# Products that nobody reads on TensorE in front of the steps of a mixture-of-experts routing

## The chip, the cores and the metric

The kernel runs on one core of a Trainium2 chip. The metric is the device time of one execution, in microseconds (us). Five engines of the core work side by side, each through its own queue in order: TensorE (PE, with its weight loads as PEld), VectorE (DVE), ScalarE (ACT), GpSimd (POOL) and SyncE (SP, which issues most transfers). The profile also records the clock that was granted to TensorE, as a share of full speed.

## The reference, cut to what matters

The input is two images of 256 channels and 56 x 56 points. Two layers follow each other. Layer 0 is windowed attention and a mixture of experts, layer 1 two 3 x 3 convolutions with ternary weights and batch norms, and again a mixture of experts. The change stands between the convolutions and the experts of layer 1, where the 6272 points are tokens:

```python
x = x + _L1_conv_ref(_ln_c(x), ...)   # ends in relu(out1 + out2)
t = _to_tokens(x)
t = t + _L1_ffn_ref(_ln_t(t), ...)

def _L1_ffn_ref(x, gate_w, gate_b, W1, b1, W2, b2):
    logits = xf @ gate_w + gate_b            # 256 -> 8 experts
    probs = softmax(logits)
    top2_vals, top2_idx = top_k(probs, 2)
    # per expert: gelu(x W1 + b1) W2 + b2, 256 -> 512 -> 256, weighted and summed
```

## The kernel before

The image is worked in 14 strips of eight rows (`STRIPS`), 448 points each. For tokens, strips stand in groups of 128: an even strip has three groups, an odd one four (`groups_of`), 49 groups in all.

Layer 1's routing takes a strip through these steps, and an order written out by hand (`all_strips`) places the steps of three strips in each round, the new one `i`, the young one `i - 1` and the old one `i - 2`. The engines PE, DVE, ACT and SP keep that order.

- `residual(i)`: DVE scales and adds (line 2208), ACT applies the ReLU into `nr` (2211), PE transposes `nr` into the PSUM tile `pt` (2221), six or eight instructions. In the next round DVE adds the tokens kept from before (2225) and leaves the strip as tokens.
- `norm(i)`: DVE takes statistics of each token (739 to 749), ACT makes the normalised rows `u` (762), PE transposes `u` into `pu` (810), ACT copies that into `ut` (813), and PE multiplies `ut` with the gate into `pl` (822): 128 x 8 products, two instructions for each of the two halves of a group's channels, 12 or 16 a strip. In the next round DVE adds the gate's bias and has the logits `lgs` (831).
- `settle(batch)`: DVE finds the two best experts of each token (857 to 876), writes them as `hots` (882), and PE counts with a few small products into `rk` how many tokens came before to the same expert (892 to 895). In the next round DVE makes the places of the rows from it (904 to 911), and POOL scatters each group's rows into `xs` in DRAM, two indirect transfers a group (929). Strips 0 to 4 are settled one by one, the later ones two at a time: `BATCHES = [[0], [1], [2], [3], [4], [5, 6], [7, 8], [9, 10], [11, 12], [13]]`.

On PE the order of one round is therefore `pt` of the new strip, `rk` of the old one, `pu` and `pl` of the young one. On DVE it is 2225 and statistics of the young strip, places of the batch settled in the last round, 2208 of the new strip, then `lgs` and the choice for the old one.

POOL sends the rows of strips 0 to 8 within the stage. When these 31 groups are out, a tiny transfer on POOL's queue (`some`, 2236) serves as a fence; SP waits for it and then loads rows of `xs` as tiles `xg` (1129). The plan of the first expert tiles and the counting for the later ones (`counts`, 985) stand in the same order on PE and DVE. The experts follow: PE transposes `xg` (1150) and multiplies with the experts' weights (`ph`, 1182, and `py`, 1201).

The PSUM pool of the stage has two buffers of each tag: `aux` for `pu`, `rk` and counts (one bank each), `pl` (one bank each) and `pt` (two banks each).[...]

`all_w` is a constant 128 x 128 bf16 tile of ones.

Of the kernel before, what the change touches and what calls it, by code (L numbers as in the profile page):

```python
# [11 lines left out]
F32 = mybir.dt.float32  # L12
# [9 lines left out]
P = 128  # L22
# [19 lines left out]
E = 8  # L42
TT = NQ
NTT = NT // TT
# [30 lines left out]
def groups_of(i):  # L75

    at = 2 * NT // P * (i // 2) + NT // P * (i % 2)
    return at, NT // P + i % 2
# [13 lines left out]
def bcast(ap, axis, shape):  # L92
    return ap.unsqueeze(axis).to_broadcast(shape)
# [551 lines left out]
def metaformer(ctx: ExitStack, tc: tile.TileContext, a: dict, out: bass.AP, flag):  # L645
    nc = tc.nc
# [71 lines left out]
    all_w = const.tile([P, P], BF16, tag="all_w", name="all_w")  # L718
# [9 lines left out]
    def token_stats(tp, src, eps, root):  # L728

        rows, n = src.shape[0], src.shape[1]  # L730

        def small(name, *more):
            bufs = None if name == "t_stats" else 3
            t = tp.tile([P, NTT, *more], F32, tag=name, name=name, bufs=bufs)
            return t[:rows, :n]

        stats, mv = small("t_stats", 6), small("t_mv", 2)
        for t in range(n):
            nc.vector.bn_stats(stats[:, t, :], src[:, t, :])  # L739
        for t in range(n):  # L740
            nc.vector.bn_aggr(mv[:, t, :], stats[:, t, :])
        rstd, nmr = small("t_rstd"), small("t_nmr")
        nc.vector.tensor_scalar_mul(nmr, mv[:, :, 0], -1.0)
        if root:
            nc.scalar.activation(rstd, mv[:, :, 1], AF.Sqrt, bias=eps[:rows])
        yield
        if root:
            nc.vector.reciprocal(rstd, rstd)
            nc.vector.tensor_tensor(nmr, nmr, rstd, ALU.mult)
        else:  # L750
            nc.gpsimd.tensor_tensor(
                rstd, mv[:, :, 1], eps[:rows].to_broadcast([rows, n]), ALU.add
            )
            nc.gpsimd.tensor_tensor(rstd, rstd, minus_half[:rows, :n], ALU.pow)
            nc.gpsimd.tensor_tensor(nmr, nmr, rstd, ALU.mult)
            yield
            yield
        return rstd, nmr
# [13 lines left out]
    def routing(layer, wp, tp, ps):  # L772
# [10 lines left out]
        wgt = rt.tile([P, TOP, NGR], F32, tag="wgt", name="wgt", bufs=2)  # L783
# [3 lines left out]
        seen_b4 = wp.tile([P, E], BF16, tag="seen_b4", name="seen_b4")  # L787
        counted, sent, held_counts = [], [], []
        small_eng = nc.gpsimd if layer == 0 else nc.vector
        rows = {}  # L790

        def norm(i, src, late=False):


            eng = nc.vector if late else small_eng
            rstd, nmr = yield from token_stats(tp, src, eps5, layer == 1 or late)
            g0, ng = groups_of(i)
            row = tp.tile([P, NTT, RW], F32, tag="u", name="u", bufs=U_BUFS[layer])
            row = rows[i] = row[:, :ng]
            u = row[:, :, :C]  # L800
            if layer == 0 or i >= FIRST[1]:
                eng.memset(row[:, :, R_EX + 1 :], 0.0)
                eng.tensor_copy(row[:, :, R_ID], ids[:, g0 : g0 + ng])
            scaled(u, src, rstd, nmr)
            yield
            ut = tp.tile([P, KC, NTT * P], F32, tag="ut", name="ut", bufs=1)
            for k in range(KC):
                pu = ps.tile([P, 512], F32, tag="aux", name="pu")
                for t in range(ng):
                    nc.tensor.transpose(  # L810
                        pu[:, t * P : (t + 1) * P], u[:, t, k * P : (k + 1) * P], ident
                    )
                nc.scalar.copy(ut[:, k, : ng * P], pu[:, : ng * P])  # L813
            if layer == 0:
                eng.tensor_tensor(src, src, u, ALU.add)
                nc.sync.dma_start(by_token(x_mid, i), src)
                yield
            lg = lgs[:, g0 : g0 + ng, :]
            pl = ps.tile([P, NTT, E], F32, tag="pl" if layer else "aux", name="pl")[:, :ng]
            for t in range(ng):  # L820
                for k in range(KC):
                    nc.tensor.matmul(  # L822
                        pl[:, t, :],
                        ut[:, k, t * P : (t + 1) * P],
                        gate[:, k, :],
                        start=k == 0,
                        stop=k == KC - 1,
                    )
            if layer == 1:
                yield  # L830
                nc.vector.tensor_tensor(lg, pl, bcast(gate_b, 1, [P, ng, E]), ALU.add)
            else:
                nc.vector.tensor_copy(lg, pl)
            yield

        def settle(strips):
# [3 lines left out]
            n = sum(groups_of(i)[1] for i in strips)  # L840
# [47 lines left out]
            if strips[-1] == FIRST[layer] - 1:  # L888
                nc.vector.tensor_copy(seen_b4, seen)
                counted.append(True)  # L890
            rk = ps.tile([P, n, E], F32, tag="aux", name="rk")
            nc.tensor.matmul(rk, before_w, hots, start=True, stop=False)
            nc.tensor.matmul(rk, all_w, bcast(seen_b, 1, full), start=False, stop=n == 1)
            for t in range(n - 1):
# [4 lines left out]
                    start=False,  # L899
                    stop=t == n - 2,  # L900
# [182 lines left out]
            nc.vector.tensor_tensor(held, below, since, ALU.mult)  # L1083
            return where, held, name

        return norm, settle, tiles, planning, gates, wgt, counted, sent

    def experts(layer, FF, plans, ys, wp, tp, ps, at_tile=None):

# [208 lines left out]
    def ring(i):  # L1298

        at = P // 2 * (1 - i % 2)  # L1300
        return slice(at, at + NT)
# [124 lines left out]
    with ExitStack() as st:  # L1426
        aw = st.enter_context(tc.tile_pool(name="att_w", bufs=1, reuse_waits="tile"))
        tp = st.enter_context(tc.tile_pool(name="att_t", bufs=2, reuse_waits="tile"))
        ps = st.enter_context(tc.tile_pool(name="att_ps", bufs=2, space=PSUM, reuse_waits="tile"))
# [38 lines left out]
        for n in "vo":  # L1468
            rows = P if n == "o" else TT
# [26 lines left out]
        for i in range(3):  # L1496
            t = sw.tile([TT, NTT, PAIRS, 4, HD], F32, tag=f"vals{i}", name=f"vals{i}")
            nc.gpsimd.memset(t[:, :, :, 1:3, :], 1.0)
            vals.append(t)
        keys = {}  # L1500
        norm0, settle0, tiles0, _, gates0, wgt0, counted0, sent0 = routing(0, aw, tp, ps)

        def project(g):
            s = g % NS
# [334 lines left out]
    with mid:  # L1839

        with ExitStack() as st:
            rp = st.enter_context(tc.tile_pool(name="raw", bufs=1, reuse_waits="tile"))
            ps = st.enter_context(tc.tile_pool(name="conv_ps", bufs=4, space=PSUM, reuse_waits="tile"))
# [9 lines left out]
            tp = strips_on.enter_context(  # L1853
                tc.tile_pool(name="conv_t", bufs=2, side="right", reuse_waits="tile")
            )
# [322 lines left out]
        with ExitStack() as both:  # L2178
# [3 lines left out]
            wp = both.enter_context(  # L2182
                tc.tile_pool(name="route_w1", bufs=1, side="right", reuse_waits="tile")
            )
            tp = both.enter_context(
                tc.tile_pool(name="route_t1", bufs=2, side="right", reuse_waits="tile")
            )
            route_ps = ExitStack()
            ps = Banks(
                route_ps.enter_context(  # L2190
                    tc.tile_pool(name="route_ps1", bufs=2, space=PSUM, reuse_waits="tile")
                ),
                True,
            )
# [3 lines left out]
            def residual(i):  # L2198

                b, s = STRIPS[i]  # L2200
                r = X[b, s]
                ng = groups_of(i)[1]
                cols = ring(i)
                back = tp.tile([P, NTT, C], F32, tag="back", name="back", bufs=1)[:, :ng]
                nc.sync.dma_start(back, by_token(x_mid, i))
                for o in range(KC):
                    ro = r[:, o, :].rearrange("p (h w) -> p h w", w=W)
                    nc.vector.scalar_tensor_tensor(  # L2208
                        ro, ro, scale2[:, o : o + 1], inner(b, s)[:, :, o], ALU.mult, ALU.add
                    )  # L2210
                    nc.scalar.activation(
                        in_blocks(nr[:, o, cols]),
                        narrow(ro),
                        AF.Relu,
                        bias=shift2[:, o : o + 1],
                    )
                pt = ps.tile([P, NTT, C], F32, tag="pt", name="pt")[:, :ng]
                for t in range(ng):
                    at = in_ring(i, t)
                    for k in range(KC):  # L2220
                        nc.tensor.transpose(  # L2221
                            pt[:, t, k * P : (k + 1) * P], nr[:, k, at], ident
                        )
                yield
                nc.vector.tensor_tensor(XT[b, s], pt, back, ALU.add)  # L2225
# [2 lines left out]
                yield from residual(i)  # L2228
                yield from norm(i, XT[STRIPS[i]])

            norm, settle, tiles, planning, gates, wgt1, _, sent = routing(1, wp, tp, ps)

            def fence():

# [107 lines left out]
    with ExitStack() as st:  # L2342
        tp = st.enter_context(tc.tile_pool(name="last_t", bufs=2, reuse_waits="tile"))
        ps = st.enter_context(tc.tile_pool(name="last_ps", bufs=2, space=PSUM, reuse_waits="tile"))
        PT = 2
        outs = {}
        for i, (b, s) in enumerate(STRIPS):
            xt = XT[b, s]
            g0, ng = groups_of(i)
            outs[i] = tp.tile([P, KC, NT], F32, tag="out", name="o_out", bufs=6)  # L2350
            rows = by_token(ys[1], i, TOP)
            for t0 in range(0, ng, PT):
# [4 lines left out]
                for t in range(t0, t0 + m):  # L2357
                    n = g0 + t
# [148 lines left out]
```

## Time and profile before

| | us |
|---|---|
| median of three runs | 1736.08 (1735.79 to 1740.23) |
| the profiled execution | 1717.51 |
| its span in the profile | 1715.70 |
| last convolution's last product on PE starts | 1116.11 |
| routing of layer 1, up to the first transpose of the experts | 1118 to 1262.16 |
| experts of layer 1 | 1262 to 1655 |
| combining and output | 1655 to 1715.7 |

All times inside the profile are counted from the start of its span. A row of the timeline gives the start, the length, the engine, the line of the kernel, the operation, and in square brackets the idle time before it and what ended it. A row of stages or windows gives the stretch, its length, for PE, weight loads, DVE, ACT and POOL the busy time and the number of instructions, then TensorE's granted clock (1.00 is full), the busy share of the DMA engines and GB/s. A row of the waits says which engine and line waited for which, in us in total, how often, and the longest.

### The profile page before, as it was taken

The page shows a single profiled execution, that of the slowest core. Times are in us where ns is not written, and L with a number is a line of the kernel's source. Part 1 is how long each engine was busy: PE and PEld are TensorE (multiplying, and loading weights), DVE is VectorE, ACT ScalarE, POOL GpSimd, SP SyncE. Part 2 cuts the span into 40 slices and gives each one's busy share as a digit, 9 for nine tenths or more (in the row PEclk, how much of TensorE's full clock was granted, in tenths as well). Part 3 has the DMA queues.
Part 4 walks back from the last instruction along what each step waited for, and adds up shares of the span by engine and source line. Part 5 has one row for each costly group of instructions (what it writes and reads, how often), then busy time and mean ns, then how long its engine had stood idle before and what let it go on. Part 6 is the DMA issues. An engine that isn't in the chain of part 4 may idle for free. (4 is left out here: it accounts for less than half of the span.)

```text
span 1715.7 us, 25578 instructions
## 1 busy us (share of the span) xinstructions
PE 1494.3 (87%) x8445; PEld 1170.3 (68%) x8445; DVE 958.2 (56%) x2620; ACT 694.3 (40%) x1419; POOL 636.9 (37%) x729
## 2 busy tenths in 40 slices
PE   5999999899877979994989879957679999999964
PEld 3556565555556857783778778746578888898952
DVE  3456667466645445976998888777743112111136
ACT  2545443353433434553444263234433334343423
POOL 2112435243343773551333323427715542222210
PEclk9999998899889989996999989955579999999975
DMA  7122324121267877984441000024457877888858
GB/s 240 47 64 92 109 96 141 46 92 62 64 180 238 296 251 290 310 302 182 175 143 71 1 1 0 10 65 140 154 186 271 274 259 263 284 288 293 299 194 328
DMA packets 94189, 291.78 MB, mean 170 GB/s; under 512 B 20183, under 2 KB 35643, under 8 KB 84960
## 3 DMA queue, kind: packets, MB, share of 16 engines
q1 hardware_dynamic: 70384, 231.82, 40.9%
q0 software_dynamic: 19856, 51.82, 8.0%
q10 hardware_dynamic: 3808, 6.42, 1.0%
q8 instruction: 69, 1.13, 0.3%
q14 instruction: 72, 0.59, 0.1%
HBM read 218.55 MB, written 74.20 MB: 171 GB/s over the span
## 5 line engine op out<-in xcount | busy, mean ns | idle before, releaser
L1182 PE MATMUL ph<-ut,w 128*128 128x256 f32 (+1 forms) x1472 | 307.7, 360 | 13.0 <-DMA w<-in_L_experts 11.0
L1211 DVE TENSOR_TENSOR y<-py,w 128x512 f32<-128x512 f32 (+1 forms) x120 | 76.9, 640 | 403.8 <-PE py L1201 387.6
L1201 PE MATMUL py<-w,h 128*128 128x256 f32 x1288 | 298.3, 380 | 2.1 <-DVE y L1211 2.1
L1182 PEld LDWEIGHTS ph<-ut,w 128*128 128x128 f32 x1472 | 250.0, 194 | 41.6 <-DMA w<-in_L_experts 12.9
L1201 PEld LDWEIGHTS py<-w,h 128*128 128x128 f32 x1288 | 243.7, 191 | 35.0 <-DVE y L1211 2.5
L929 POOL DMA_INDIRECT xs<-u,pos x196 | 195.4, 997 | 114.7 <-issue 37.5
L1213 POOL DMA_INDIRECT ys<-y,dest x136 | 136.0, 1000 | 217.5 <-DVE dest L1157 94.8
L1189 ACT ACTIVATE h<-ph,w 128x256 f32<-128x256 f32 (+1 forms) x368 | 162.7, 448 | 110.0 <-PE ph L1182 104.5
L1592 ACT ACTIVATE ex<-sc 112x476 f32<-112x476 f32 (+3 forms) x224 | 116.8, 573 | 176.0 <-PE sc L1582 174.7
L1154 ACT COPY ut<-pt 128x512 f32<-128x512 f32 (+1 forms) x120 | 65.2, 543 | 272.8 <-PE pt L1150 272.8
L1923 PE MATMUL pc<-lo,wq 128*128 128x448 f32 x336 | 133.7, 400 | 5.7 <-DVE lo L1898 5.5
L1923 PE MATMUL pc<-hi,wq 128*128 128x448 f32 x336 | 132.5, 396 | 2.4 <-DVE x L1945 1.9
L1612 DVE TENSOR_TENSOR acc<-av,acc 128x238 f32<-128x238 f32 (+3 forms) x224 | 88.4, 408 | 77.4 <-PE av L1602 76.6
L1213 POOL DMA_INDIRECT ys<-y,to x81 | 81.6, 1008 | 121.3 <-DVE dest L1157 63.5
L1602 PE MATMUL av<-ex,vals 112*64 112x238 f32 (+3 forms) x896 | 122.8, 397 | 4.1 <-DVE acc L1612 4.1
L2066 PE MATMUL pc<-hi,wq 128*128 128x448 f32 (+1 forms) x288 | 102.9, 367 | 17.8 <-ACT hi L2033 9.4
L1573 PE MATMUL sc<-q_im,keys 32*112 32x238 f32 (+3 forms) x896 | 99.3, 426 | 8.7 <-ACT ex L1592 8.6
L2066 PE MATMUL pc<-lo,wq 128*128 128x448 f32 (+1 forms) x288 | 102.1, 364 | 0.2 <-DVE lo L2034 0.2
L1896 POOL TENSOR_TENSOR v<-pad 128x928 f32<-128x928 f32 (+1 forms) x28 | 56.8, 2041 | 105.1 <-ACT pad L1879 61.0
L1602 PEld LDWEIGHTS av<-ex,vals 112*64 112x64 f32 x896 | 56.1, 140 | 52.0 <-issue 27.9
L1150 PE MATMUL pt<-ident,xg 128*128 128x128 f32 x434 | 69.6, 281 | 21.6 <-DMA xg<-xs 17.9
L1573 PEld LDWEIGHTS sc<-q_im,keys 32*112 32x112 f32 x896 | 46.0, 175 | 49.7 <-ACT ex L1592 25.3
(279 smaller groups left out, 2477.3 us busy)
## 6 DMA issues: line engine op xcount, KB each, us to landing
w<-in_L_experts SPq DMA_DIRECT2D x64, 1154.0 KB
w<-in_L_experts SPq DMA_DIRECT2D x56, 641.0 KB
xg<-xs SPq DMA_DIRECT2D x97, 260.0 KB
acc<-in_fresh SPq DMA_DIRECT2D x14, 896.0 KB
got<-ys SPq DMA_DIRECT2D x21, 512.0 KB
got<-ys SPq DMA_DIRECT2D x7, 1024.0 KB
xt<-in_x_tok SPq DMA_DIRECT2D x14, 448.0 KB
rec<-shares SPq DMA_DIRECT2D x28, 224.0 KB
```

The costliest lines, as they stand in the source:

```text
L929: w = nc.gpsimd.indirect_dma_start(xs[:, :], bass.IndirectOffsetOnAxis(ap=pos[:, j, t0 + t : t0 + t + 1], axis=0), at_of[t][0][:, at_of[t] ...
L1182: nc.tensor.matmul(ph[:, :g], w1[:, k, f * P : (f + 1) * P], d["ut"][:, k, :g], start=k == 0, stop=k == KC - 1,)
L1189: nc.scalar.activation(d["h"][:, f, :g], ph[:, :g], AF.Gelu, bias=b1[:, f : f + 1])
L1201: nc.tensor.matmul(py[:, i, :], d["h"][:, f, i * P : (i + 1) * P], w2[:, f, :], start=f == 0, stop=f == NF - 1,)
L1211: nc.vector.tensor_tensor(y[:, :gp], py[:, :gp], bcast(b2, 1, [P, gp, C]), ALU.add)
L1213: o = nc.gpsimd.indirect_dma_start(ys[:, :], bass.IndirectOffsetOnAxis(ap=d["to"][:, i : i + 1], axis=0), y[:, i, :], None, bounds_check=T ...
L1573: nc.tensor.matmul(sc[h // 2][:, h % 2, :nq], keys[g][p, c, tx * TT : (tx + 1) * TT], q_im[p, c, r0:r1, c0:c1], start=True, stop=False,)
L1592: nc.scalar.activation(e[:, :, :nq], sc[j][:, :, :nq], AF.Exp, scale=HD**-0.5)
L1602: nc.tensor.matmul(av[VW * i : VW * (i + 1), :nq], vals[g % 3][:, tx, 2 * c + j, 2 * i : 2 * i + 2, :].rearrange("p a d -> p (a d)"), ex[j ...
L1612: added = nc.vector.tensor_tensor(d, av[:, :nq].rearrange("p (h w) -> p h w", w=c1 - c0), d, ALU.add)
L1923: nc.tensor.matmul(pc[:, :NT], wq[:, k, c, dx * C + o * P : dx * C + (o + 1) * P], part[:, :, k, dx : dx + W], start=m == 0, stop=m == 2 * ...
L2066: nc.tensor.matmul(pc[:, : 2 * ns * W], wq[:, k, c, dx * C + o * P : dx * C + (o + 1) * P], part[:, : 2 * ns, k, dx : dx + W], start=m == ...
```

## The change

Within layer 1's routing a helper `busy(n)` puts `n` products of `all_w` with itself, repeated to 512 columns, into PE's queue. They are written to a tile `spare` of one PSUM bank, which nobody reads. The helper is called in front of `pt` (30 for strip 0, 6 for each other strip), in front of `pu` (20 for strip 0, else 5), in front of `pl` (2), and in front of `rk` (12 for the first batch, else 4). To make room for the bank, `pl` has one buffer in place of two in layer 1. Layer 0 is left as it was. On the other four engines the instructions and their order are the same as before.

```diff
+        def busy(n):
+
+            if layer == 0:
+                return
+            if not spare:
+                spare.append(ps.tile([P, NTT, P], F32, tag="spare", name="spare", bufs=1))
+            for _ in range(n):
+                nc.tensor.matmul(
+                    spare[0], all_w, bcast(all_w, 1, [P, NTT, P]), start=True, stop=True
+                )
...
             scaled(u, src, rstd, nmr)
             yield
+            busy(5 if i else 20)
             ut = tp.tile([P, KC, NTT * P], F32, tag="ut", name="ut", bufs=1)
...
             lg = lgs[:, g0 : g0 + ng, :]
-            pl = ps.tile([P, NTT, E], F32, tag="pl" if layer else "aux", name="pl")[:, :ng]
+            busy(2)
+            if layer:
+                pl = ps.tile([P, NTT, E], F32, tag="pl", name="pl", bufs=1)[:, :ng]
+            else:
+                pl = ps.tile([P, NTT, E], F32, tag="aux", name="pl")[:, :ng]
...
+            busy(4 if strips[0] else 12)
             rk = ps.tile([P, n, E], F32, tag="aux", name="rk")
...
+                busy(6 if i else 30)
                 pt = ps.tile([P, NTT, C], F32, tag="pt", name="pt")[:, :ng]
```

## Prediction

> **What bounds the kernel now.** I read the page's forty slices first, then engine sums by stage, the granted clock in windows cut at its own edges, the timelines of TensorE (PE) and VectorE (DVE), and the waits. Slices:
>
> ```profile
> PE   5999999899877979994989879957679999999964
> PEclk9999998899889989996999989955579999999975
> ```
>
> Around slices 26 to 29 stands layer 1's routing, the one long stretch with a half clock and a half-filled PE. By stage (columns: length; busy PE, weight load, DVE, ACT, POOL; clock; DMA):
>
> ```profile
> 1118.00:1262.00 144.00, 90.69 (x452) 77.46 (x452) 106.40 (x434) 60.83 (x120) 74.58 (x154) 0.56 0.42 138
> 1262.00:1655.00 393.00, 389.56 (x2075) 346.82 (x2075) 70.62 (x257) 146.60 (x325) 138.61 (x141) 0.99 0.76 260
> ```
>
> The experts after it are PE from end to end at clock 0.99, so what the routing gains or loses moves the end of the kernel one for one. In the routing DVE is busier than PE. What DVE waits for, and how the stage ends:
>
> ```profile
> DVE lgs L831 <- PE pl L822: 12.9, 6, 4.8
> DVE x L2225 <- PE pt L2221: 5.0, 3, 1.7
> DVE counts L987 <- PE counts L985: 3.0, 1, 3.0
> ...
> 1247.36 0.61 POOL L2236 DMA_DIRECT2D some<-xs  x1 [7.17 <-DMA xs<-u,pos]
> ...
> 1252.96 4.78 SPq L1129 DMA_DIRECT2D xg<-xs  x5
> ...
> 1262.11 0.19 PE L985 MATMUL counts<-seen_all,all_w 128*128 128x8 bf16 x1 [0.88 <-DVE seen_all L983]
> 1262.16 1.95 PE L1150 MATMUL pt<-ident,xg 128*128 128x128 f32 x8
> ```
>
> So in the 112 us of the first three rows a faster PE can return at most 20.9 us. Two paths end in the first expert tile: the strip loop, whose last step (counts) lets PE go at 1262.1, and POOL's scattered rows, the fence and the loads of xg, issued at 1252.96 and, at 260 KB each, due about 1256. The strip loop is last, by some 6 us: gains beyond that are covered by POOL's path unless it starts earlier too.
>
> **What the clock follows.** Four windows of 3.41 us:
>
> ```profile
> 1184.19:1187.60 3.41, 3.41 (x18) 3.41 (x17) 0.98 (x2) 1.05 (x3) 2.61 (x6) 0.50 0.25 87
> 1187.60:1191.02 3.42, 1.93 (x14) 1.49 (x12) 3.35 (x12) 1.43 (x4) 2.84 (x6) 1.00 0.69 222
> 1191.02:1194.43 3.41, 1.80 (x6) 1.11 (x6) 2.96 (x16) 2.85 (x6) 2.83 (x9) 0.50 0.25 87
> ...
> 1163.71:1167.12 3.41, 3.41 (x18) 3.41 (x18) 1.39 (x7) 2.67 (x5) 2.83 (x6) 0.50 0.49 190
> ```
>
> Both 1163.7 and 1184.2 show PE busy throughout, but only the second is followed by the full clock. The first is mostly pl, matmuls of 8 columns; the second is transposes of 128. Counting moved columns only (pl is then 1/16 of a transpose), the windows of the routing that were followed by the full clock held 0.75 of activity or more, those that stayed low 0.60 or less, and the full clock was lost after windows of 0.08 or less; elsewhere in the trace it held from about 0.4 up and mostly went below that. That count is my estimate from shapes and times.
>
> The page "TensorE: Matmul & The Clock Gate" of the Trainium skill has two rules on this. Its closing table ("Why this matters for your kernels") says that throughput is kept if PE has no idle gap above about 3 us. The change fills such gaps; by that rule the clock would stay full and my sum would end near -4 us. The rows speak against it: the window at 1187.6 had a gap of 1.7 us only, the rest was pl, and the clock went. "Part 4: PE-mode transpose" says that transposes don't engage the full clock; then only the new products count, 17 x 0.22 = 3.7 us in some 9 us a strip, and it would be low most of the time (+20 us). Here transposes alone, 1184.8 to 1187.6, did engage it. I count transposes, and not pl.
>
> **The change, part by part.** It adds 269 products of 512 bf16 columns: in front of pt 30 + 13x6, of pu 20 + 13x5, of pl 14x2, of rk 12 + 9x4. DVE, ACT, POOL and SP keep the same instructions in the same order, and no DMA is added. Price of one: ph (256 f32 columns) takes 3.46/16 = 0.216 us at full clock; a conv product of 448 columns starts every 0.22 us, which scaled to 512 is 0.25. I take 0.22, and 0.43 at half clock; the other end adds 1 us to what follows.
>
> The single pl buffer costs nothing: pl of strip i stands behind rk on PE, and rk waits for DVE's hots, which DVE makes after it has read the pl before. Without that cover it would be a wait of some 3 us a strip. The first product waits for a DVE read of the last convolution that ended at 1116.7; PE is free at 1116.5.
>
> *First strips.*
>
> ```profile
> 1124.82 1.93 PE L2221 MATMUL pt<-ident,nr 128*128 128x128 f32 x6 [8.34 <-ACT nr L2211]
> 1132.09 2.31 PE L2221 MATMUL pt<-ident,nr 128*128 128x128 f32 x8 [5.35 <-ACT nr L2211]
> 1134.20 1.49 PE L810 MATMUL pu<-ident,u 128*128 128x128 f32 x6
> 1135.61 1.97 PE L822 MATMUL pl<-gate,ut 128*128 128x8 f32 x12
> ...
> 1141.87 0.20 PE L892 MATMUL rk<-hots,before_w 128*128 128x24 bf16 x1 [0.99 <-DVE hots L882]
> ```
>
> The 30 fit the gap of 8.3 us (6.6 us, done 1123.3): free, and pt of strip 0 runs warm, 0.7 us earlier. The six of strip 1 run at once and are over at 1127.3; PE then idles 4 us for nr until 1131.4, so whatever the windows' phase one lies mostly in that gap and the clock drops. Now the 20 stand between pt(1) and pu(0), where there was no gap: u was ready at 1131.1. pt(1) ends near 1133.6, five or six products run at half clock until a full window has passed, the rest at full: pu(0) starts near 1139.0 instead of 1134.2 (1137 at full clock). It and pl are faster, but pl(0) ends at 1142.2 against 1137.6; then the six (1.3), pt(2) (0.7) and the 12 (2.6) put rk(0) at 1146.8, +4.9. DVE's place, and behind it on DVE all of strips 1 and 2, and POOL's first rows, wait for it. Some comes back in strip 1: +4.2 remains on both DVE and POOL.
>
> *Later strips.* Strips of four groups matter, since pl is longest there:
>
> ```profile
> 1181.77 3.15 PE L822 MATMUL pl<-gate,ut 128*128 128x8 f32 x14 [0.45 <-ACT ut L813]
> 1184.77 1.95 PE L2221 MATMUL pt<-ident,nr 128*128 128x128 f32 x8
> ...
> 1184.95 0.19 DVE L831 TENSOR_TENSOR lgs<-pl,gate_b 128x32 f32<-128x32 f32 x1 [1.87 <-PE pl L822]
> 1186.81 1.23 DVE L2225 TENSOR_TENSOR x<-pt,back 128x1024 f32<-128x1024 f32 x1 [1.66 <-PE pt L2221]
> ```
>
> From hots to the end of pl PE needs 6.9 us now. Warm: rk 0.25, five products 1.1, pu 0.44, ut 0.8, pu 0.44, ut 0.8 (the two products hide in it), pl 16 x 0.128 = 2.05 (0.128 from ten in 1.28 us at clock 1.00): 5.9, a gain of 1.0. Then six products and pt take 1.3 + 0.9, against 1.9: a loss of 0.4 for the DVE step that waits for pt. Net -0.6 where strips go in pairs (four such pairs), -1.2 for each two strips of the single batches, where pt is not waited for. But ut's wait and pl together are 2.5 us of little activity, so a window of 3.41 us over them holds 0.26 to 0.4, and I find that for some 70% of the phases. If the clock drops for one window behind pl, the six and pt run at half speed just where DVE waits: +1.2 for that pair; if it drops inside pl, for two windows, +2.6. Weights 0.24, 0.48, 0.28: about +1.2 a pair, +5 for four; about 0 for the single batches. Counts come 1 us sooner. The last chain, hots to pl of strip 13, gains 1.0 warm and loses 2 cold: -0.5.
>
> **Sum** on the profiled execution: 4.2 + 5 - 1 - 0.5 = +7.7, call it +7. That execution took 1717.51 us (span 1715.70 and 1.81 around it), 18.6 us below the median of the runs shown; I carry the difference in us to that median: 1743.
>
> **The rivals.** (1) The clock holds from the first strip on, since pl counts for more when full clock is kept than it did for getting it: start +2.5, pairs -2.4, singles -2.5, counts and end -2: -4.5 us, 1731.5, not slower. For it: windows down to 0.4 held. It decides if windows of 0.26 hold as well. Against it: the loss of clock after 1187.6, with pl in it. (2) The clock stays low through most of the stage, so that each strip carries 17 x 0.43 = 7.3 us of products on top of 7.9 of its own, more than DVE's 8: with the clock low for half of the windows about +20, 1756. For it: the 0.75 needed to return. Against it: with products PE is dense outside pl, so a return takes a window or two. (3) POOL decides: its 31 groups of rows at 2.9 us are 89 us from the first rank on, and xg comes when they are out. If the start is hardly later and the loop faster, only the 6 us between the paths can come in, and with a start 3 to 4 us late most of that is gone: 1733 to 1738. (4) The products fill only gaps that were idle anyway and nothing moves: 1736; against it, pu had no idle time in front of it.
>
> **How the numbers follow.** About 0.3% (5.2 us) is what a measurement of this kernel can tell from no change. My forecast (+3 to +12) 0.45, of it two thirds slower by more; rival 1 0.22, a third of it faster by more; rival 2 0.18, slower; rivals 3 and 4 0.15, no change. Slower 0.50, within 0.40, faster 0.10 with a little added for a start that costs nothing. Range 1731 (rival 1) to 1756 (rival 2).
>
> **What would show it.** Right: pu of strip 0 starts 4 to 5 us later after the convolution's end; rk of strip 0 likewise; clock windows between 0.7 and 0.9 over the stage, with 0.50 behind long pl stretches; DVE's wait for pt grows above 5.0 us while that for pl falls below 12.9; the first expert transpose comes some 7 us later. Wrong: a mean clock above 0.95 with the transpose before 1262 (rival 1), or below 0.7 (rival 2).

## The result: 0.65% slower, and the profile after

| | before | changed |
|---|---|---|
| median, 22 runs each in turn | 1735.25 us | 1748.74 us |
| lowest to highest | 1726.66 to 1747.85 | 1732.54 to 1760.78 |
| the profiled execution | 1717.51 | 1752.46 |

The ratio is 1.0065, with a 95% interval of 1.0046 to 1.0084: slower by more than the 0.3% that can be told from no change, by some 11 us, or 13.5 us between the medians. The measurements of this case fall into two groups, one with the kernel before near 1717 us and one with it at 1735 to 1746, so every ratio below compares runs made side by side on one chip, and stages are compared from the start of the last convolution product. The last point matters at once: the profile of before is of the first group, that of the changed kernel of the second; the two spans (1715.70 and 1750.7) differ by 35.0 us, but 20.6 of that lie ahead of the first changed instruction (that product starts at 1116.11 before and at 1136.71 after). The stage from there to the first expert transpose took 146.05 us before and 159.37 after, +13.3. The rest is +1.1.

The slices of the changed kernel's page, in tenths:

```profile
PE   5999998999878878894989879988789999999964
PEclk9999999999789998996999989989879999999985
```

The hollow in slices 26 to 29 (counted from 0), where PE was at 5 to 7 and the clock at 5 to 7, is filled to 7 or 8 and to 7 to 9. PE is busier and faster there, and the kernel is slower. The changed kernel by stage (length, then busy time of PE, weight load, DVE, ACT and POOL, then clock):

```profile
1136.71:1296.08 159.37, 127.37 (x724) 81.81 (x723) 108.95 (x437) 59.33 (x120) 74.45 (x155) 0.84 0.39 130
1296.08:1690.20 394.12, 389.98 (x2075) 346.97 (x2075) 70.58 (x256) 146.48 (x325) 138.90 (x141) 0.99 0.75 257
```

DVE is busy for 108.95 us, as in the kernel before (108.43 us from the same starting point, in the profile of the run "before again" below), in a longer stage, so it waits for longer. The experts take as long in either kernel (393 and 394 us). PE's timeline of the changed kernel shows how the stage starts:

```profile
1137.32 6.63 PE L799 MATMUL spare<-all_w 128*128 128x512 bf16 x30 [0.23 <-DVE x L2101]
1146.63 2.50 PE L799 MATMUL spare<-all_w 128*128 128x512 bf16 x6
1152.15 2.31 PE L2239 MATMUL pt<-ident,nr 128*128 128x128 f32 x8 [3.01 <-ACT nr L2228]
1154.26 5.91 PE L799 MATMUL spare<-all_w 128*128 128x512 bf16 x20
1160.00 0.82 PE L822 MATMUL pu<-ident,u 128*128 128x128 f32 x6
1161.09 1.64 PE L838 MATMUL pl<-gate,ut 128*128 128x8 f32 x12
1164.53 2.75 PE L799 MATMUL spare<-all_w 128*128 128x512 bf16 x12
1167.12 0.18 PE L909 MATMUL rk<-hots,before_w 128*128 128x24 bf16 x1
```

The 30 run in a gap and cost nothing. The 20 have no gap: the last row before `pu` is theirs, and no bracket shows idle time. `pu` of strip 0 starts 23.29 us after the convolution product, 18.09 before: +5.2. `rk` of strip 0 is at 30.41, 25.76 before: +4.6. After that it follows no simple line: it had come down to +2.3 at strip 3, was +6.4 at strip 4, came down to +5.1 to +5.3 by strip 10, and was +12.3 at strips 11 and 12. Both rises begin in the same way. At strip 4, in the changed kernel (first two rows) and in a later profile of the same kernel, "changed, third" below (last two):

```profile
1193.45 0.49 PE L822 MATMUL pu<-ident,u 128*128 128x128 f32 x3
1195.84 0.48 ACT L825 COPY ut<-pu 128x384 f32<-128x384 f32 x1 [5.22 <-remote]
...
1175.74 0.49 PE L822 MATMUL pu<-ident,u 128*128 128x128 f32 x3
1176.27 0.48 ACT L825 COPY ut<-pu 128x384 f32<-128x384 f32 x1 [3.35 <-PE pu L822]
```

ACT copied `pu` 0.04 us after it was over in the second case and 1.9 us after it in the first. PE then idled 2.4 us, and the clock fell for two windows (1198 to 1205). The second rise, in the changed kernel's PE, DVE and ACT timelines around 1262 us:

```profile
1261.71 0.29 PE L912 MATMUL rk<-hots,all_w 128*128 128x48 bf16 x6
1261.86 1.24 PE L799 MATMUL spare<-all_w 128*128 128x512 bf16 x5
1262.94 0.60 PE L822 MATMUL pu<-ident,u 128*128 128x128 f32 x4
1268.49 1.11 PE L822 MATMUL pu<-ident,u 128*128 128x128 f32 x4 [4.96 <-ACT ut L825]
...
1265.62 0.22 DVE L921 TENSOR_TENSOR place<-rk,tabs 128x56 f32<-128x56 f32 x1 [1.13 <-remote]
...
1267.85 0.58 ACT L825 COPY ut<-pu 128x512 f32<-128x512 f32 x1 [7.49 <-remote]
```

`rk` was over at 1262.0, but DVE's `place`, which needs it, started 3.6 us later. The first half of `pu` was over at 1263.5, and ACT copied it at 1267.85, 4.3 us later. These releases carry the name "remote": the profile found no instruction at that moment which gave them. PE then stood idle for 4.96 us, in front of work that was delayed by its own results arriving late; the clock went with it. The prediction has no such step.

### The profile page after: what moved, and what is told of

Same layout as the page of the kernel before. It is cut to its first block, busy times and chain, and to the rows that moved or that the text cites. A ratio compares the mean times of both kernels' runs of the same rounds, so it can differ in the third digit from the quotient of the medians.

```text
span 1750.7 us, 26120 instructions
## 1 busy us (share of the span) xinstructions
PE 1544.8 (88%) x8714; PEld 1181.5 (67%) x8714; DVE 959.2 (55%) x2620; ACT 691.3 (39%) x1419; POOL 635.5 (36%) x729
## 5 line engine op out<-in xcount | busy, mean ns | idle before, releaser
L1199 PE MATMUL ph<-ut,w 128*128 128x256 f32 (+1 forms) x1472 | 313.1, 364 | 17.6 <-DMA w<-in_L_experts 11.7
L1199 PEld LDWEIGHTS ph<-ut,w 128*128 128x128 f32 x1472 | 252.6, 196 | 48.0 <-DMA w<-in_L_experts 13.3
L1619 PE MATMUL av<-ex,vals 112*64 112x238 f32 (+3 forms) x896 | 126.7, 406 | 4.1 <-DVE acc L1629 4.1
L1167 PEld LDWEIGHTS pt<-ident,xg 128*128 128x128 f32 x434 | 56.2, 147 | 36.8 <-ACT ut L1171 14.4
```

The lines of the kernel that those rows point to most:

```text
L1167: nc.tensor.transpose(pt[:, k, i * P : (i + 1) * P], d["xg"][:, i, k * P : (k + 1) * P], ident)
L1199: nc.tensor.matmul(ph[:, :g], w1[:, k, f * P : (f + 1) * P], d["ut"][:, k, :g], start=k == 0, stop=k == KC - 1,)
L1619: nc.tensor.matmul(av[VW * i : VW * (i + 1), :nq], vals[g % 3][:, tx, 2 * c + j, 2 * i : 2 * i + 2, :].rearrange("p a d -> p (a d)"), ex[j ...
```

## The experiments

Each table row of counts gives what stands in front of `pt`, `pu`, `pl` and `rk` in the later strips and, behind the bar, in strip 0 or the first batch; the changed kernel is 6|30, 5|20, 2|2, 4|12. "Before" is the median of the kernel before, measured beside it. "Stage" is the length from the last convolution product to the first expert transpose in the one profile of that kernel, and the clock is that of the same stretch.

| kernel | counts | before | ratio | stage | clock in it |
|---|---|---|---|---|---|
| one pl | none | 1717.23 | 0.9998 [0.9975, 1.0020] | 146.42 | 0.53 |
| first only | 0\|30, 0\|20, 0\|2, 0\|12 | 1717.23 | 1.0008 [0.9994, 1.0022] | 148.41 | 0.60 |
| later only | 6\|0, 5\|0, 2\|0, 4\|0 | 1717.23 | 0.9979 [0.9959, 0.9999] | 145.66 | 0.82 |
| not before pu | 6\|30, 0, 2, 4 | 1717.23 | 0.9968 [0.9950, 0.9987] | 137.64 | 0.87 |
| changed again | as changed | 1746.10 | 1.0099 [1.0067, 1.0131] | 169.31 | 0.84 |
| short start | 6\|30, 5, 2, 4 | 1746.10 | 1.0037 [1.0014, 1.0060] | 157.42 | 0.85 |
| only pu | 0, 5\|20, 0, 0 | 1746.10 | 1.0061 [1.0034, 1.0089] | 167.41 | 0.60 |
| half columns | as changed, 256 columns | 1746.10 | 1.0049 [1.0026, 1.0072] | 161.77 | 0.69 |
| before again | the kernel before | 1717.30 | 0.9997 [0.9978, 1.0016] | 146.17 | 0.52 |
| changed, third | as changed | 1717.30 | 1.0024 [1.0010, 1.0038] | 146.78 | 0.92 |
| not before pu, again | 6\|30, 0, 2, 4 | 1717.30 | 0.9960 [0.9943, 0.9976] | 138.87 | 0.84 |
| sixteen columns | as changed, 16 columns | 1717.30 | 1.0020 [1.0001, 1.0038] | 148.13 | 0.56 |

Rows with the same time of before were measured side by side, as one set; the three sets ran on three chips.

**One buffer for the logits, no products.**

```diff
-            busy(5 if i else 20)
+            busy(0)
```

and so at the other three places.

> No added products at all, only the single pl buffer. If the cost comes from the products (my theory): ratio 1.000, and the stretch from the last convolution product to the first expert transpose stays within 2 us of the 146.1 us of before. Rival, the buffer itself makes pl wait for the logits: about +3 us a strip, ratio above 1.01, and PE waits for DVE's lgs show up.

Measured 0.9998, stage 146.42. The second `pl` buffer was worth nothing, so all that follows is the products.

**Only the first strip's products, and only the later ones.**

```diff
-            busy(5 if i else 20)
+            busy(5 if i else 0)
```

for "later only", and `busy(0 if i else 20)` for "first only"; the other places alike.

> Only the products of strip 0 and of the first batch (30, 20, 2, 12). Theory that the start costs most of what is steadily lost: pu of strip 0 about 5 us later after the last convolution product (18.1 before), rank of strip 0 about 4.6 us later, and most of it stays to the end of the stage: +4 us. Rival, the later products carry the loss (stalls and half clock from strip 5 on, 7 of the 13 us in the changed kernel's profile): this one then shows less than +2 us at the end, because the later strips win it back where VectorE waited for TensorE.

> No products in strip 0 and in the first batch, the rest as changed. Theory that later products cost about what they bring: stage within -3 to +3 us of before, ratio 0.998 to 1.002. Rival, they cost on their own (stretched semaphore updates of TensorE near strip 11, half clock behind pl): +6 to +9 us, ratio 1.004 or more.

First only: stage +2.4, between the theory's +4 and the rival's less than +2, and 1.0008. `pu` of strip 0 started at 23.16 us, as late as in the changed kernel; over the stage half of those 5 us came back. Later only: 0.9979 with the stage at -0.4. So the later strips' products do not lose time by themselves, which is against the prediction's +5. The two parts sum to about nothing in this set, where the changed kernel measured 1.0065 in its own: the first sign that the two groups of measurements differ by more than an offset.

**No products in front of `pu`.**

```diff
-            busy(5 if i else 20)
+            busy(0)
...
-            busy(4 if strips[0] else 12)
+            busy(4)
```

> As changed, without the products in front of pu (20 and 5) and with 4 instead of 12 in front of the first rank. pu stands straight behind rk on the path that VectorE waits for. Theory: the start costs nothing, hots to end of pl falls from 6.9 to about 4.9 us in strips of four groups, VectorE's wait for pl (12.9 us) falls below 6: stage 4 to 8 us shorter than before, ratio 0.996 or below. Rival, without these products the clock is not held (activity too low behind pl), so pl stays slow: stage within 3 us of before.

0.9968, the stage shorter by 8.4 us, at clock 0.87: faster than the kernel before, by just over the 0.3%. Two things were taken out together, the products in front of `pu` and eight of those in front of the first `rk`; no run separates them.

**The changed kernel again, a short start, products in front of `pu` alone, half the columns.** These ran as one set, on a chip where the kernel before took 1746.1 us.

```diff
-            busy(5 if i else 20)
+            busy(5)
...
-            busy(4 if strips[0] else 12)
+            busy(4)
```

is the short start; "only pu" sets the other three places to 0; for half the columns:

```diff
-                    spare[0], all_w, bcast(all_w, 1, [P, NTT, P]), start=True, stop=True
+                    spare[0][:, :2], all_w, bcast(all_w, 1, [P, 2, P]), start=True, stop=True
```

> The changed kernel as it is, beside the variants. In the first measurement it was 11 us slower, and its profile lost 5 us at the start and 7 us near strip 11, where semaphore updates of TensorE came 4 us after its products; neither the products of strip 0 alone (+2.4 us of stage, ratio 1.0008) nor the later ones alone (-0.4 us, 0.9979) show that. Theory A, the loss is the start and what the later strips don't win back: stage +2 to +6 us, ratio 1.001 to 1.004, no such delay. Theory B, the late updates belong to this kernel: stage +10 to +14 us, ratio 1.006 or more, and the delay stands again in its waits.

> As changed, but 5 instead of 20 in front of the first pu and 4 instead of 12 in front of the first rk. If the long runs at strip 0 are what is lost at the start (they stand where there was no gap), pu of strip 0 comes within 1 us of before, and the stage is 3 to 5 us shorter than that of the changed kernel run beside it. Rival, the later products in front of pu are what costs: less than 2 us shorter.

> Only the products in front of pu (20 and 5), none elsewhere. Theory: they lie on the path from hots to pl and without the others don't hold the clock, so each strip pays up to 2.1 us at half clock, VectorE's wait for pl rises from 12.9 to about 20 us: stage 8 to 14 us longer, ratio 1.004 to 1.008. Rival, they too are hidden in TensorE's idle time: within 2 us of before.

> As changed, with 256 columns in each product instead of 512. Each costs half as long and adds half the activity. Theory of activity by columns: the clock drops after most stretches of pl (mean clock of the stage near 0.7, against 0.8 to 0.85), the start loses about 2 us instead of 4.6, stage within -2 to +3 us of before. Rival, the clock follows instructions and not columns: mean clock as with 512 columns, stage 3 to 6 us shorter than before.

The changed kernel came out at 1.0099, more than in its first measurement and on theory B's side. The short start takes 11 to 12 us off that (1.0037; the medians are 1764.83 and 1752.91), where 3 to 5 were expected. `pu`'s products alone give 1.0061, as expected (the stage of their profile is 21 us above 146, where 8 to 14 were expected): they lift the clock no further than 0.60 and stand in front of operands that are ready. Half columns, at half the price, reach only 0.69 and still lose (1.0049), which was not expected.

What the four have in common is in the waits. These are rows of the changed kernel in that set, over the stage (which engine and line waited for which, us in total, times, longest):

```profile
ACT ut L825 <- remote: 23.0, 3, 8.2
DVE counts L1004 <- remote: 10.6, 1, 10.6
DVE lgs L847 <- PE pl L838: 11.8, 7, 4.9
```

And in the first profile of the changed kernel, over its whole span:

```profile
DVE y L1228 <- remote: 19.8, 4, 7.6
ACT ut L825 <- remote: 13.8, 3, 7.5
ACT ut L1171 <- remote: 10.8, 1, 10.8
ACT h L1206 <- remote: 5.0, 1, 5.0
```

Lines 1171, 1206 and 1228 are in the experts, which the change doesn't touch; the waiting engines wait there for PE too. Seven of this profile's ten such waits stand between 580 and 643 us, in the experts and the routing of layer 0, and the first added product starts at 1137.32. One instruction of layer 0's experts in the kernel before, then in the changed one with the products of PE that it waits for:

```profile
573.36 0.69 DVE L1211 TENSOR_TENSOR y<-py,w 128x512 f32<-128x512 f32 x1 [1.39 <-PE py L1201]
...
573.65 1.89 PE L1218 MATMUL py<-w,h 128*128 128x256 f32 x8
580.17 0.69 DVE L1228 TENSOR_TENSOR y<-py,w 128x512 f32<-128x512 f32 x1 [5.97 <-remote]
```

`py` was over at 575.54, and DVE had it 4.6 us later. So the added products, which come half a millisecond later, can't be what makes these releases. All five profiles of kernels with products in the 1735 and 1746 group have such rows in that stretch, and none of the eight experiments' profiles in the 1717 group has one, nor has the profile of before shown ahead of the prediction, an execution of 1717.51 us. Set against that profile instruction by instruction, the five fall behind by 14.7 to 15.2 us between its 580 and its 600 us, the eight by at most 1.9. Most of the 18 to 29 us between the groups thus arise in code that both kernels share, which makes it likely, though no profile shows it, that the kernel before has late releases there too.

In the stage itself "changed again" has five, half columns four, the short start two and "only pu" none. The four stages exceed the 146 us of before, known from other chips alone, by 11 to 23 us, but the medians exceed before's by only 7 to 19, in each of the four by 4 to 10 us less than the stage. So the kernel before's own stage was probably longer in this set as well; that is an estimate from one profile of each. Of the 11.9 us between the stages of "changed again" and of the short start, 4.8 are there at the first `rk`; how much of the rest belongs to the shorter start, and how much to five late releases against two, can't be told.

**The kernel before and the changed one once more, the version without `pu`'s products once more, and products of sixteen columns.** Was it the chip's group, and not the kernel, that made the late releases? And is it the number of instructions or their length that costs?

```diff
-                    spare[0], all_w, bcast(all_w, 1, [P, NTT, P]), start=True, stop=True
+                    spare[0][:, 0, :16], all_w, all_w[:, :16], start=True, stop=True
```

> The kernel before, for a profile of it beside the others of this call: e5 to e8 were measured beside runs of before at 1746 us, e1 to e4 beside runs at 1717 us, and only the first set shows late semaphore updates of TensorE in its profiles. If the lateness belongs to the execution and not to the products, this profile has it too wherever the time is near 1740, and then a stage of 150 to 155 us instead of 146. If it belongs to the products, the stage is 146 us at any time.

> The changed kernel beside the two others. Start: pu of strip 0 at 22 to 24 us after the last convolution product (18.1 before), as in the two profiles so far. If this call runs near 1717: stage 0 to +4 us against before (the start less what later strips win), ratio 1.000 to 1.003. If near 1740: +10 us or more, ratio 1.006 to 1.010, as in the two measurements so far.

> e4 once more, to see whether its gain holds beside the changed kernel[...]. Theory: its gain is on the path hots to pl[...]: ratio 0.995 to 0.998 in both. Rival: near 1740 late updates eat it: 0.999 to 1.003.

> As changed, with 16 columns in each product: the same number of instructions and of instruction fetches, next to no time in the array. If the cost is array time on the path: start within 1 us of before, clock as before (0.55 to 0.6), ratio 0.999 to 1.001. If it is the number of instructions: start and stage as in the changed kernel, ratio 1.004 or more.

This set fell into the group near 1717. The kernel before gave 0.9997 against itself, which shows what an interval here is worth. The changed kernel gave 1.0024, inside the 0.3%, with no late release in its profile and a stage of 146.78 us, 0.7 longer than before. The rows of the stage of the kernel before and of the changed one, then those of the version without `pu`'s products, and of the sixteen columns:

```profile
1113.55:1259.72 146.17, 97.33 (x456) 83.50 (x454) 108.43 (x437) 60.81 (x120) 74.58 (x155) 0.52 0.41 136
1119.11:1265.89 146.78, 120.68 (x725) 77.26 (x723) 108.64 (x437) 59.62 (x120) 75.30 (x155) 0.92 0.40 136
```

```profile
1118.40:1257.27 138.87, 108.52 (x631) 74.01 (x630) 108.29 (x437) 60.61 (x120) 74.00 (x155) 0.84 0.42 142
```

```profile
1108.39:1256.52 148.13, 100.53 (x725) 90.23 (x723) 108.65 (x437) 60.72 (x120) 75.10 (x155) 0.56 0.41 135
```

Clock 0.92 with 146.78 us, 0.84 with 138.87: a higher clock by itself doesn't make the stage shorter, for what raises it stands in the way. The waits of the kernel before for `pt` over this stretch, in the profile shown ahead of the prediction (there the rows count from a later start), and those of the changed kernel in this set:

```profile
DVE x L2225 <- PE pt L2221: 8.4, 4, 3.4
...
DVE x L2243 <- PE pt L2239: 11.7, 4, 4.1
DVE lgs L847 <- PE pl L838: 7.7, 5, 4.9
DVE counts L1004 <- PE counts L1002: 1.6, 1, 1.6
```

and of the version without `pu`'s products:

```profile
DVE x L2243 <- PE pt L2239: 9.0, 3, 4.1
DVE lgs L847 <- PE pl L838: 6.3, 2, 5.0
DVE counts L1004 <- PE counts L1002: 0.8, 2, 0.6
```

Over the same stretch the kernel before waited 8.4 us for `pt`, 12.9 for `pl` and 3.0 for `counts`, 24.3 in all. The changed kernel waits 21.0 there, 3.3 less, and has lost 3.5 at the start: nothing is left. Without `pu`'s products the three come to 16.1, 8.2 less, and the stage is shorter by 7.3. Most of the difference is the start: in that version `rk` of strip 0 is 25.2 us behind the convolution product, in the changed kernel 30.3. The sixteen columns warm next to nothing (0.56 against 0.52) and the stage is 2.0 us longer, or about 7 ns for each of the 269 instructions: start and clock are those of the first theory, the ratio of 1.0020 is neither's. The net loss of the full products in this set (1.0024) can't be told from that: these cost more at the start, where sixteen columns make `pu` of strip 0 only 0.6 us later, and earn most of it back by the clock.

## Why the prediction was right, and where not

The sign and the size held: 1743 predicted, 1748.74 measured, +7 against +11 to +13.5. The sum behind it was right in its first term, and the total came near by luck. In the third run of the changed kernel, whose profile has no late release, the stage was 0.7 us longer, not 7: +3.5 from the start, -2.9 from the later strips. In the first measurement's profile two rises of 4.1 and 6.9 us that begin with late releases, which the working doesn't have, stand where it had +5 for another reason.

- *The start, +4.9 at the first `rk` and +4.2 left behind it: right.* Measured +4.6 and then +3.6 at strips 1 and 2 (+4.5 and +3.5 in the third run). `pu` of strip 0 was 5.1 to 5.2 us later (predicted 4.8). The 20 in front of it took 5.91 us, 5.39 in the third run of the changed kernel: the clock had dropped in the gap before `pt` of strip 1, as the working said. "First only" shows the same lateness by itself.
- *30 in front of the first `pt`, the single `pl` buffer: free, right.* They took 6.63 us of a gap; one product is 0.22 us at full clock, the value taken.
- *Later strips, +5 for four pairs and about 0 for the single batches: wrong in sign.* This is the step that failed. In the changed kernel without late releases the loss at the start, 3.5 us at strips 1 and 2, was 2.0 at the `rk` of strip 4 and 0.6 at that of strips 11 and 12. Strips 3 and 4, settled one by one, gained 1.5 us (warm value of the working: -1.2), and the four pairs 1.4, about 0.3 a pair (warm value: -0.6, forecast +1.2). What was mis-sized is the weight of 70% for a dropped clock. By the same count of moved columns, the clock held in the stage from about 0.38 and was lost at about 0.35 and below; the bigger error was to expect 0.26 to 0.4 in most windows over `pl`. In the first profile, of 16 windows at full clock from 1181 to 1242 two fell to 0.34 or less, and the others had 0.43 and more. The mean clock was 0.92 in the third run and 0.84 in the first; "between 0.7 and 0.9" holds for the first measurement and not for the third run.
- *The rows for it.* Four windows of the changed kernel's first profile, from edge to edge of the clock's own grid:

```profile
1215.17:1218.59 3.42, 3.02 (x19) 1.80 (x18) 3.28 (x16) 1.83 (x4) 2.75 (x7) 1.00 0.59 193
1194.69:1198.11 3.42, 1.47 (x11) 1.23 (x11) 3.28 (x15) 1.38 (x4) 2.81 (x6) 1.00 0.71 227
1239.06:1242.47 3.41, 2.61 (x21) 2.13 (x20) 2.33 (x12) 1.37 (x3) 2.61 (x6) 1.00 0.76 221
1201.52:1204.93 3.41, 3.41 (x12) 2.05 (x11) 2.49 (x10) 0.00 (x0) 2.83 (x6) 0.50 0.23 79
```

  My estimate of the moved columns' share is 0.43, 0.23, 0.34 and 1.00. After the first the clock stayed full, after the second and third it fell, after the fourth it came back. The second is the window of the late release at strip 4. The third had PE busy for 2.61 of 3.41 us and lost the clock all the same, because half of that, 1.29 us, was `pl`. The rule of the Trainium skill ("TensorE: Matmul & The Clock Gate", "Why this matters for your kernels"), no idle gap above about 3 us, doesn't see this window, whose idle time is 0.80 us in all. The prediction was right to set it aside, and too strict in what it set in its place.
- *Some 11 us of the stage's +13.3 in the first profile, 4.1 at strip 4 and 6.9 behind strip 10: not in the working at all.* They begin with late releases, and the clock was lost behind them (1198 to 1205 and 1266.4 to 1276.6). Such releases stand long before the first product as well, and only in the 1735 and 1746 group, where the changed kernel cost 1.0065 and 1.0099; in the group without them it cost 1.0024. That they take part in the loss is seen in the timelines above; what makes them, whether they hit the stage of the kernel before as often, and so how much of the 1.0065 is theirs, stays open: no profile of before was taken in that group. A shorter start helped by 11 us there, while the 23 products it leaves out last 5 us at full clock; that was measured once and is not explained.
- *Counts -1, last chain -0.5.* DVE's wait for counts fell from 3.0 to 1.6 us in the third run; in the first profile it was 3.0 as before. The last chain was not measured by itself.
- *Signs.* In the third run DVE's wait for `pt` rose and for `pl` fell, as announced (8.4 to 11.7, and 12.9 to 7.7). In the first profile that for `pt` rose to 11.8, and that for `pl` stayed at 12.9. The first expert transpose 7 us later: 13.3 and 0.7 in two profiles, so it met neither.
- *Rival 1 (the clock holds, -4.5)* was half right: in the later strips it does hold, but the start isn't cheaper. With the start's products taken away ("later only") it measured 0.9979, where the rival had 0.9974; without the products in front of every `pu` it measured 0.9968 and 0.9960.
- *Rival 2 (clock mostly low, products in the way)* did not come in the changed kernel (0.84 and 0.92), but "only pu" is it: clock 0.60, the wait for `pl` 19.0 us in all, 1.0061, in a stage without a late release.
- *Rival 3 (POOL's path covers the gain)* didn't decide. In the version without `pu`'s products SP issued the loads at 1248.91 and PE began the experts at 1257.27:

```profile
1248.91 4.79 SPq L1146 DMA_DIRECT2D xg<-xs  x5
...
1257.17 0.19 PE L1002 MATMUL counts<-seen_all,all_w 128*128 128x8 bf16 x1 [0.88 <-DVE seen_all L1000]
1257.27 1.94 PE L1167 MATMUL pt<-ident,xg 128*128 128x128 f32 x8
```

  The distance is 8.4 us, 9.2 before. Both paths moved up together, since POOL waits for places that DVE now has sooner; the strip loop still ends last.
- *Rival 4 (only idle gaps are filled, nothing moves)* is out: `pu` of strip 0 came 5.1 to 5.2 us later.
- *Not settled:* in the third run the whole kernel was 4.1 us above before's median (5.5 between the medians of the set), while its profiled stage was only 0.7 longer. One profile against medians can't tell where the other 3 to 5 us lie.

## What to carry to other kernels

Products that keep TensorE's clock up belong where the engine waits anyway (here the gap in front of `pt`), not between a ready operand and the instruction that a busier engine is waiting for: on one chip the kernel gave 0.9960 without the products in front of `pu` (and with 4 in place of 12 in front of the first `rk`), and 1.0024 with them. Judge whether the clock will hold by moved columns in each 3.4 us window, not by the busy time of the row, and judge the change by the waits of the engine that bounds the stage: here a higher mean clock went with a longer stage. When measurements of the same kernels give different ratios, look in the waits for rows that name no instruction, and look for them ahead of the changed code too, before explaining the difference from the code.

## What the runs showed of the hardware that was not expected

- Releases of TensorE's results came 1.9 to 4.6 us after the end of its instruction in the rows above (waits that end in this way lasted up to 13.8 us), in all five profiles of the 1735 and 1746 group, and in none of the nine of the other. In those five they are there from 590 us at the latest, ahead of all added products, and go with 15 us lost in 20 us of layer 0's experts. All five are of kernels with products, so a profile of before in that group is what is missing.
- The clock's changes all fell on a grid of 3.41 us; it came back after windows with some 0.75 or more of moved columns, stayed low below that, held from about 0.38, and was lost at about 0.35 or less (counted from shapes and times in the stages of the traces, an estimate that is good to some 0.02).
- Products of 16 columns, 269 of them, left the mean clock of the stage at 0.56 (0.52 without); of 256 columns at 0.69; of 512 at 0.84 to 0.92.
